# One fold for two units of attention in a graph-transformer kernel, and half of a weight matrix loaded behind the first input

## The chip, the cores and the metric

The kernel runs on one core of a Trainium2 chip. The metric is device time in microseconds of one launch; lower is better. The core's engines work side by side, each through its own instructions in order: TensorE (PE in the profile, its weight loads PEld) multiplies matrices into PSUM, VectorE (DVE) and ScalarE (ACT) work on elements and can read PSUM, [...], and SyncE (SP) issues nearly all DMA transfers. They wait for each other through semaphores.

## The reference, cut to what matters

For each of 16 samples, x has 1024 nodes of 256 channels; adj is a 1024 x 1024 matrix that all samples share. All is fp32.

```python
# layer 0: x = layernorm(x + attention)
c = mean(x, channels); A = 2 * abs(abs(sigmoid(c_j - c_i) - .5) - .5)
g = relu((x.T @ (adj * A)) * para)      # 256 x 1024: the queries, 4 heads of 64
k, v = split(x @ kv_w)
out = softmax(q @ k.T * scale) @ v
# layer 1: x = layernorm(x + (x + h) / 2)
h = relu(x @ w1_loop + adj @ (x @ w1_neigh) + b1)      # 128 wide
h = relu(h @ w2_loop + adj @ (h @ w2_neigh) + b2)      # 256 wide
```

The change touches the softmax's denominator: out is a sum over nodes of exp(score) * v, divided by the sum of the exponentials.

## The kernel before, in words

The loop over samples b (L1021) is a pipeline written out by hand: while sample b is in attention, the queries, keys and values of b+1 are made, the first graph convolution of b-1 and the second of b-2 run joined in one product, and the result of b-3 is normalized and stored. The order of the program text is the order of each engine's instructions (`tc.manual_schedule()`). Graph products, keys and values use a seven-product scheme in place of eight (a Strassen form), whose operands are sums and differences made by VectorE and GpSimd.

Attention (class at L602) of a sample is cut into four units: two pairs of heads by two halves of the nodes (512 queries). For a unit u:

- `scores(u)` (L616): eight tiles of keys, for each two matmuls (one for each head of the pair, L624) and one exp on ScalarE (L627, tile pr, 128 x 1024). VectorE adds the eight pr into acc (L631, L633), transposes it in blocks of 32 (L635, accB) and reduces it to den_part, 128 x 32 (L637). What is left is a sum over groups of partitions.
- `outputs(u)` (L639): sixteen matmuls of v with pr into one PSUM bank (av, L644), and a transpose into the tile o (L648).
- `add(u)` (L650): one matmul of the constant matrix `fold` with den_part (L656) finishes the sum for all partitions; two reciprocals, one for each head (L660); o times them (L662); o added to the residual stream xB (L664); sums of xB for the coming layer norm (L665). The last unit also joins these sums (L255) and takes the extremes of the reciprocals (L668, L669).

Where `add` stands differs by sample. With `both`, that is for samples 2 to 14, add(0) comes between scores(1) and outputs(1), ahead of the sums for the keys (L1081); add(1) after the second of seven graph products of the joined convolution (L1057, `between[2]`); add(2) after `c2.last()` and ahead of scores(3) (L1074); add(3) in the middle of step 1 of the query graph (L1147). Samples 0, 1 and 15 take them one unit later each, in the loop at L1091 or at set places.

After add(3) the same sample goes on with `norm.mean` in the middle of step 2 (fold of the sums on TensorE, L251; mean and subtraction on VectorE, L307 and L310), `norm.squares` (ScalarE, L315), and behind these `q.end` (L578): ScalarE copies the first of seven query products out of PSUM (L585), VectorE adds them up (L586 and on). Pair 3 of the query graph's right sides is made by VectorE (L495, L548 to L551) between add(3) and `norm.mean`. Then `kv.run` (L408) makes the keys and values of b+1; its first product on TensorE (L401) writes the PSUM buffer that L586 reads.

SBUF tiles of 128 x 1024 share a pool of 25 slots (`row_tile`, L99); a tile that finds no free slot waits for the last reader of another. The tile o has one slot of its own, so outputs(u+1) cannot write it before add(u) has read it. den_part has two slots. PSUM has three big buffers of two banks and two single banks (L85 to L92).

At the start (L115 to L120) x of sample 0 is loaded in four pieces by SP's queue, and kv_w as a whole, 512 KB, by ScalarE's queue at the same time. GpSimd makes sums of its blocks (L131), which SP stores; the keys of sample 0 (L343) need the left half of kv_w's columns, the values (L356) the right half.

Of the kernel before, what the change touches and what calls it, by code (L numbers as in the profile page):

```python
# [10 lines left out]
F32 = mybir.dt.float32  # L11
I32 = mybir.dt.int32
AF = mybir.ActivationFunctionType
ALU = mybir.AluOpType
# [4 lines left out]
def kernel(  # L19
# [31 lines left out]
    nc = tc.nc  # L51
# [39 lines left out]
    def bank_psum(name):  # L91
        return psum.tile([P, FB], F32, tag="bank", name=name, bufs=2)  # L92
# [20 lines left out]


    x_first = xpool.tile([P, NT, C], F32, tag="x", name="x_0")  # L115
    for t0 in range(0, NT, 2):
        nc.sync.dma_start(out=x_first[:, t0:t0 + 2, :],
                          in_=x[0, t0 * P:(t0 + 2) * P, :].rearrange("(t p) c -> p t c", p=P))
    kvw_sb = const.tile([P, NC, 2 * C], F32, name="kvw_sb")
    nc.scalar.dma_start(out=kvw_sb, in_=kv_w.rearrange("(cc p) f -> p cc f", p=P))  # L120
    w1l_sb = const.tile([P, NC, HID], F32, name="w1l_sb")
    w1n_sb = const.tile([P, NC, HID], F32, name="w1n_sb")
    w2l_sb = const.tile([HID, C], F32, name="w2l_sb")
# [172 lines left out]
    def by_node(t):  # L296
        return t.rearrange("p (bn r) -> p bn r", r=S)
# [304 lines left out]
    class Attention:  # L602
# [5 lines left out]

        def __init__(self, b, xB, qT, kT, v):
            self.b, self.xB, self.qT, self.kT, self.v = b, xB, qT, kT, v  # L610
            self.part, self.o = {}, {}

            self.rden = small.tile([P, len(UNITS) * FB // S], F32, tag="rden", name=f"rden_{b}", bufs=2)
            self.sums = small.tile([P, NC, NB], F32, tag="sums", name=f"sums_{b}", bufs=2)

        def scores(self, u):  # L616

            b, (pair, j) = self.b, UNITS[u]
            self.pr = []
            for mt in range(NT):  # L620
                ps = big_psum(f"s_{b}_{u}_{mt}")
                for s in range(2):
                    rows = slice(s * HD, (s + 1) * HD)
                    nc.tensor.matmul(ps[:, ts(s, FB)], self.kT[rows, pair, ts(mt, P)], self.qT[rows, pair, ts(j, FB)],  # L624
                                     start=True, stop=True)
                pr = row_tile(f"pr_{b}_{u}_{mt}")
                nc.scalar.activation(pr, ps, AF.Exp)  # L627
                self.pr.append(pr)
                if mt == 1:
                    acc = row_tile(f"acc_{b}_{u}")  # L630
                    nc.vector.tensor_add(acc, self.pr[0], pr)  # L631
                elif mt > 1:
                    nc.vector.tensor_add(acc, acc, pr)  # L633
            accB = row_tile(f"accB_{b}_{u}")
            nc.vector.transpose(accB, acc)  # L635
            self.part[u] = small.tile([P, N // S], F32, tag="den_part", name=f"den_part_{b}_{u}", bufs=2)
            nc.vector.tensor_reduce(self.part[u], by_node(accB), AX.X, ALU.add)  # L637

        def outputs(self, u):  # L639
            b, (pair, j) = self.b, UNITS[u]  # L640
            pav = bank_psum(f"av_{b}_{u}")
            for mt in range(NT):
                for s in range(2):
                    nc.tensor.matmul(pav[s * HD:(s + 1) * HD, :],  # L644
                                     self.v[:, mt, pair * P + s * HD:pair * P + (s + 1) * HD],
                                     self.pr[mt][:, ts(s, FB)], start=(mt == 0), stop=(mt == NT - 1))
            self.o[u] = work.tile([P, FB], F32, tag="o", name=f"o_{b}_{u}")
            nc.vector.transpose(self.o[u], pav)  # L648

        def add(self, u):  # L650

            b, (pair, j) = self.b, UNITS[u]
            half = FB // S
            pd = bank_psum(f"den_ps_{b}_{u}")
            den = pd[:, 0:2 * half]
            nc.tensor.matmul(den, fold.rearrange("p a k -> p (a k)"), self.part.pop(u), start=True, stop=True)  # L656
            rden = self.rden[:, ts(u, half)]
            for s in range(2):
                rows = slice(s * HD, (s + 1) * HD)
                nc.vector.reciprocal(rden[rows, :], den[rows, ts(s, half)])  # L660
            o = by_node(self.o.pop(u))
            nc.vector.tensor_mul(o, o, rden.unsqueeze(2).to_broadcast([P, half, S]))  # L662
            dst = by_node(self.xB[pair][:, ts(j, FB)])
            nc.vector.tensor_add(dst, dst, o)  # L664
            nc.vector.tensor_reduce(self.sums[:, pair, ts(j, half)], dst, AX.X, ALU.add)  # L665
            if u == len(UNITS) - 1:
                join(self.sums)
                nc.vector.tensor_reduce(rden_min[:, b:b + 1], self.rden, AX.X, ALU.min)  # L668
                nc.vector.tensor_reduce(rden_max[:, b:b + 1], self.rden, AX.X, ALU.max)  # L669
# [293 lines left out]
    def run():  # L963
# [57 lines left out]
        for b in range(B):  # L1021
# [29 lines left out]
            def gap1():  # L1051
                for t in (0, TJ):
                    q.load(t)
                if both:
                    both.fetch(1, 4)
                    both.run({1: (lambda: q.left(nc.gpsimd),),
                              2: (lambda: att.add(1),),  # L1057
                              6: (lambda: q.likeness(0), lambda: c3 and c3.moments()),
                              7: (lambda: q.likeness(TJ),),
                              5: (weigh_first,),  # L1060
                              4: (lambda: c3 and c3.finish(out[b - 3]),),
                              3: (c1.turn_blocks,)})
                else:
                    q.left(nc.gpsimd)
                    for t in (0, TJ):
                        q.likeness(t)
                    store("01", rows01)
                    c1.first(rows01, lambda: (att.add(1), adj_sums(rows01, 1), adj_sums(rows01, 2), weigh_first()))
                    c1.turn_blocks()

            def gap2():
                if both:
                    c2.last()
                    att.add(2)  # L1074

            between = [gap0, gap1, gap2] if c1 and more else []
            if more:
# [1 line left out]
            for u in range(len(UNITS)):  # L1079
                att.scores(u)  # L1080
                if u == 1 and between:  # L1081
                    att.add(0)
                    kv = KeysValues(b + 1, ready["xT"])
                    kv.sums()
                if u == 3 and between:
                    for t in (2, TJ + 2, 3, TJ + 3):
                        q.load(t)
                    for t in (2, TJ + 2, 3, TJ + 3):
                        q.likeness(t)
                    q.right(1)  # L1090
                if u and (not between or u == 3 and not both):  # L1091
                    att.add(u - 1)
                att.outputs(u)
                if u == 2 and more:
                    if c1:
                        for t in (1, TJ + 1):
                            q.load(t)
                            q.likeness(t)
                            q.times_adj(t)
                    else:  # L1100
                        for t in range(3):
                            q.load(t)
                            q.weigh(t)
                if u < 3 and between:
                    between[u]()
                if u == 0 and more and not between:
                    means(q, xb, str(b + 1))()
# [36 lines left out]
            elif more:  # L1144
                q.pair(2)
                q.step(0)
                q.step(1, lambda: att.add(3))  # L1147
                q.pair(3)
                q.step(2, lambda: (norm.mean(), norm.squares()))
                q.load_para()  # L1150
                kv.load()
                q.step(3)
                qT = q.end(norm.sum_squares)
                xB = load_blocked(b + 1, f"a{b + 1}")
                load_next()
                kT, v = kv.run(norm.variance, q.scale)
                if not c2:
                    adj_sums(rows01, 3)
                norm.scale()
                norm.spread()  # L1160
            else:
                c2.load_h1()
                c2.load_x()
                both.fetch(2, 3)
                c1.inner()
                both.left(nc.gpsimd)
                both.fetch(1, 4)
                both.run({1: (lambda: att.add(3),), 2: (norm.mean, norm.squares, norm.sum_squares), 7: (norm.variance,),
                          5: (norm.scale, norm.spread)})
                c1.turn(0)  # L1170
                c2.last()
                c1.turn(1)
# [86 lines left out]
```

## Time and profile before

| what | value |
|---|---|
| median of 3 runs | 2161.2 us (2160.72 to 2161.49) |
| the profiled execution's own time | 2160.7 us |
| span of the profiled execution | 2158.9 us, TensorE clock 0.998 |
| TensorE busy | 2145.5 us, 8412 records (two passes for each fp32 matmul) |
| VectorE busy | 1906.0 us, 2402 instructions |
| ScalarE busy | 1040.9 us |
| GpSimd busy | 361.7 us |
| fold of the denominators, L656 | 128 records for 64 matmuls, median 276 ns |
| one sample, first key product to the next one | 132.8 us (384.86 to 517.68 us) |

A profile line gives an engine, the line of the kernel, the operation, the tiles written and read, and times. The timeline gives start and duration in us, and in brackets the idle time of that engine ahead of the instruction with what ended it. A matmul's end is modelled and lies past the start of the next one, so distances between starts are the better measure of what TensorE spends.

### The profile page before, as it was taken

The numbers are of one execution on the slowest core, as the hardware profiler recorded it, in microseconds if no ns is written. First come the engines' busy times: TensorE is split into PE (matmuls) and PEld (weight loads), VectorE is DVE, ScalarE is ACT, GpSimd is POOL, SyncE is SP. The second block draws the span as 40 slices with busy tenths as digits, with TensorE's granted clock in tenths as the row PEclk, the third lists the DMA queues.
The fourth block names the chain that finished last, engine by engine and source line by source line (L and its number), as shares of the span: only waits on it lengthen the run. The fifth ranks groups of instructions, "written<-read, shape, count | busy, mean of one in ns | idle before, by whom it ended". The sixth has DMA issues, their size and how long they took to land.

```text
span 2158.9 us, 23875 instructions
## 1 busy us (share of the span) xinstructions
PE 2145.5 (99%) x8412; PEld 1030.9 (48%) x8412; DVE 1906.0 (88%) x2402; ACT 1040.9 (48%) x1374; POOL 361.7 (17%) x201
## 2 busy tenths in 40 slices
PE   9999999999999999999999999999999999999997
PEld 5344444544445444454545445454454544544354
DVE  5999998889998899998999989999889898889964
ACT  4745545545345554445544555445553445535412
POOL 1010130311303013030120302203021130211021
PEclk9999999999999999999999999999999999999999
DMA  9493653736548364563755636555374553733443
GB/s 236 120 145 117 147 156 108 160 113 123 160 118 181 93 126 151 138 170 88 121 172 124 159 88 121 172 127 156 98 130 153 127 156 118 140 133 83 122 136 99
DMA packets 611918, 290.72 MB, mean 135 GB/s; under 512 B 504784, under 2 KB 569168, under 8 KB 611792
## 3 DMA queue, kind: packets, MB, share of 16 engines
q1 hardware_dynamic: 611520, 288.61, 54.5%
q8 instruction: 68, 1.11, 0.2%
q14 instruction: 58, 0.48, 0.1%
q10 hardware_dynamic: 272, 0.52, 0.1%
HBM read 242.35 MB, written 46.72 MB: 134 GB/s over the span
## 4 chain that ended last, share of the span: by engine, by line


## 5 line engine op out<-in xcount | busy, mean ns | idle before, releaser
L627 ACT ACTIVATE pr<-s 128x1024 f32<-128x1024 f32 x512 | 476.1, 1054 | 183.8 <-PE s L624 183.0
L633 DVE TENSOR_TENSOR acc<-acc,pr 128x1024 f32<-128x1024 f32 x384 | 498.9, 1299 | 41.1 <-DVE acc L633 1.0
L624 PE MATMUL s<-qT,kT 64*128 64x512 f32 x2048 | 456.8, 596 | 0.0
L644 PE MATMUL av<-pr,v 128*64 128x512 f32 x2048 | 453.6, 595 | 0.0
L624 PEld LDWEIGHTS s<-qT,kT 64*128 64x128 f32 x2048 | 191.5, 186 | 232.9 <-ACT pr L627 112.8
L327 POOL TENSOR_TENSOR rstd<-rstd,neg_half 128x32 f32<-128x32 f32 x16 | 99.8, 6238 | 1129.8 <-DVE rstd L325 615.6
L644 PEld LDWEIGHTS av<-pr,v 128*64 128x64 f32 x2048 | 141.3, 137 | 289.3 <-issue 274.3
L489 ACT ACTIVATE wg<-c_row,c_col 128x1024 f32<-128x1024 f32 x128 | 147.0, 1148 | 69.1 <-DVE accB L635 50.5
L495 DVE SCALAR_TENSOR_TENSOR wg<-wg,adj 128x1024 f32<-128x1024 f32 x128 | 150.0, 1210 | 12.0 <-ACT wg L490 12.0
L922 PE MATMUL hu_ps<-adj,R 128*128 128x512 f32 x360 | 158.3, 596 | 0.0
L490 ACT ACTIVATE wg<-wg 128x1024 f32<-128x1024 f32 x128 | 135.4, 1058 | 4.1
L315 ACT ACTIVATE sq<-xB_a 128x1024 f32<-128x1024 f32 x32 | 33.8, 1057 | 197.0 <-DVE xB_a L310 195.7
L576 PE MATMUL g_ps<-wg,S 128*128 128x512 f32 x224 | 116.7, 603 | 0.0
L576 PE MATMUL g_ps<-T,S 128*128 128x512 f32 x224 | 114.4, 592 | 0.0
L576 PE MATMUL g_ps<-wg,x 128*128 128x512 f32 x224 | 109.0, 599 | 0.0
L922 PE MATMUL hu_ps<-adjT,t 128*128 128x512 f32 x240 | 105.7, 592 | 0.0
L922 PEld LDWEIGHTS hu_ps<-adj,R 128*128 128x128 f32 x360 | 67.3, 190 | 78.9 <-issue 78.7
L631 DVE TENSOR_TENSOR acc<-pr,pr 128x1024 f32<-128x1024 f32 x64 | 83.2, 1300 | 23.8 <-ACT pr L627 23.8
L938 ACT COPY snap<-hu_ps 128x512 f32<-128x512 f32 x15 | 8.8, 585 | 154.6 <-PE hu_ps L922 150.5
L635 DVE STREAM_TRANSPOSE accB<-acc 128x1024 f32<-128x1024 f32 x64 | 79.7, 1245 | 3.5 <-DVE acc L633 0.5
L637 DVE TENSOR_REDUCE den_part<-accB 128x32 f32<-128x1024 f32 x64 | 78.1, 1220 | 2.2
L810 PE MATMUL h_ps<-w2n_sb,uT 128*128 128x256 f32 x240 | 72.7, 385 | 0.0
(204 smaller groups left out, 3001.8 us busy)
## 6 DMA issues: line engine op xcount, KB each, us to landing
adj<-in_adj_dram SPq DMA_DIRECT2D x128, 512.0 KB, 4.6
adj<-adjT SPq DMA_DIRECT2D x120, 512.0 KB, 10.2
para<-in_L_gnn_para_dram SPq DMA_DIRECT2D x32, 512.0 KB, 3.5
xB_a<-in_x_dram SPq DMA_DIRECT2D x128, 128.0 KB, 4.3
x1d<-xB_a SPq DMA_DIRECT2D x128, 128.0 KB, 3.4
x<-x1d SPq DMA_DIRECT2D x16, 1024.0 KB, 15.0
xB<-in_x_dram SPq DMA_DIRECT2D x120, 128.0 KB, 4.7
x<-in_x_dram SPq DMA_DIRECT2D x15, 1024.0 KB, 6.4
```

Source lines behind the costliest of these rows:

```text
L327: nc.gpsimd.tensor_tensor(self.rstd, self.rstd, neg_half, ALU.pow)
L489: nc.scalar.activation(wg, self.c_row, AF.Abs, bias=self.c_col[:, t:t + 1], scale=-1.0)
L490: nc.scalar.activation(wg, wg, AF.Tanh, scale=-0.5)
L495: nc.vector.scalar_tensor_tensor(wg, wg, 1.0, self.adj.pop(t), op0=ALU.add, op1=ALU.mult)
L576: nc.tensor.matmul(self.p[n], x_n[:, k, :], w_n, start=(k == 0), stop=(k == TJ - 1))
L624: nc.tensor.matmul(ps[:, ts(s, FB)], self.kT[rows, pair, ts(mt, P)], self.qT[rows, pair, ts(j, FB)], start=True, stop=True)
L627: nc.scalar.activation(pr, ps, AF.Exp)
L631: nc.vector.tensor_add(acc, self.pr[0], pr)
L633: nc.vector.tensor_add(acc, acc, pr)
L635: nc.vector.transpose(accB, acc)
L644: nc.tensor.matmul(pav[s * HD:(s + 1) * HD, :], self.v[:, mt, pair * P + s * HD:pair * P + (s + 1) * HD], self.pr[mt][:, ts(s, FB)], start ...
L922: nc.tensor.matmul(dst, self.x[n][:, k, :], half_adj[w][:, k, :] if w else of_rows(rows, k), start=(start and k == 0), stop=(k == TJ - 1), ...
```

## The change

The fold takes two units at once, where a sample runs with the joined product (2 to 14). den_part becomes one tile for two units; add takes one or two units, with one matmul of 64 columns, two reciprocals over both units, and then per unit the product, the addition and the sums as before. add(0) and add(1) both stand where add(1) stood, add(2) and add(3) both where add(3) stood. As o of an even unit has to last longer, it moves to half of a row tile. In sample 1, add(0) now stands behind the sums for the keys. At the start kv_w is loaded in two halves: the keys' columns by ScalarE's queue as before, the values' columns by SP's queue, behind the four pieces of x.

```diff
+    kvw_sb = const.tile([P, NC, 2 * C], F32, name="kvw_sb")
     for t0 in range(0, NT, 2):
         nc.sync.dma_start(out=x_first[:, t0:t0 + 2, :],
                           in_=x[0, t0 * P:(t0 + 2) * P, :].rearrange("(t p) c -> p t c", p=P))
-    kvw_sb = const.tile([P, NC, 2 * C], F32, name="kvw_sb")
-    nc.scalar.dma_start(out=kvw_sb, in_=kv_w.rearrange("(cc p) f -> p cc f", p=P))
+    for eng, cols in (nc.scalar, slice(0, C)), (nc.sync, slice(C, 2 * C)):
+        eng.dma_start(out=kvw_sb[:, :, cols], in_=kv_w[:, cols].rearrange("(cc p) f -> p cc f", p=P))
...
-            self.part[u] = small.tile([P, N // S], F32, tag="den_part", name=f"den_part_{b}_{u}", bufs=2)
-            nc.vector.tensor_reduce(self.part[u], by_node(accB), AX.X, ALU.add)
+            if u % 2 == 0:
+                self.part = small.tile([P, 2, N // S], F32, tag="den_part", name=f"den_part_{b}_{u}", bufs=2)
+            nc.vector.tensor_reduce(self.part[:, u % 2, :], by_node(accB), AX.X, ALU.add)
+            self.parts[u] = self.part
...
-            self.o[u] = work.tile([P, FB], F32, tag="o", name=f"o_{b}_{u}")
+            name = f"o_{b}_{u}"
+            self.o[u] = work.tile([P, FB], F32, tag="o", name=name) if u % 2 else row_tile(name)[:, 0:FB]
             nc.vector.transpose(self.o[u], pav)
 
-        def add(self, u):
-
-            b, (pair, j) = self.b, UNITS[u]
-            half = FB // S
-            pd = bank_psum(f"den_ps_{b}_{u}")
-            den = pd[:, 0:2 * half]
-            nc.tensor.matmul(den, fold.rearrange("p a k -> p (a k)"), self.part.pop(u), start=True, stop=True)
-            rden = self.rden[:, ts(u, half)]
+        def add(self, *units):
+
+            b, half = self.b, FB // S
+            u0, n = units[0], len(units)
+            pd = bank_psum(f"den_ps_{b}_{u0}")
+            den = pd[:, 0:2 * half * n]
+            part = [self.parts.pop(u) for u in units][0]
+            nc.tensor.matmul(den, fold.rearrange("p a k -> p (a k)"),
+                             part[:, u0 % 2:u0 % 2 + n, :].rearrange("p u k -> p (u k)"), start=True, stop=True)
+            den = den.rearrange("p (u s h) -> p u s h", u=n, s=2)
+            rden = self.rden[:, u0 * half:(u0 + n) * half].rearrange("p (u h) -> p u h", u=n)
             for s in range(2):
                 rows = slice(s * HD, (s + 1) * HD)
-                nc.vector.reciprocal(rden[rows, :], den[rows, ts(s, half)])
-            o = by_node(self.o.pop(u))
-            nc.vector.tensor_mul(o, o, rden.unsqueeze(2).to_broadcast([P, half, S]))
-            dst = by_node(self.xB[pair][:, ts(j, FB)])
-            nc.vector.tensor_add(dst, dst, o)
-            nc.vector.tensor_reduce(self.sums[:, pair, ts(j, half)], dst, AX.X, ALU.add)
+                nc.vector.reciprocal(rden[rows], den[rows, :, s, :])
+            for k, u in enumerate(units):
+                pair, j = UNITS[u]
+                o = by_node(self.o.pop(u))
+                nc.vector.tensor_mul(o, o, rden[:, k, :].unsqueeze(2).to_broadcast([P, half, S]))
+                dst = by_node(self.xB[pair][:, ts(j, FB)])
+                nc.vector.tensor_add(dst, dst, o)
+                nc.vector.tensor_reduce(self.sums[:, pair, ts(j, half)], dst, AX.X, ALU.add)
...
-                              2: (lambda: att.add(1),),
+                              2: (lambda: att.add(0, 1),),
...
                 if both:
                     c2.last()
-                    att.add(2)
...
                 if u == 1 and between:
-                    att.add(0)
                     kv = KeysValues(b + 1, ready["xT"])
                     kv.sums()
...
-                if u and (not between or u == 3 and not both):
+                if u and (not between or u != 2 and not both):
                     att.add(u - 1)
...
-                q.step(1, lambda: att.add(3))
+                q.step(1, lambda: att.add(*((2, 3) if both else (3,))))
```

More of the change, by code (lines that the diff above doesn't have):

```diff
@@ L610, in __init__ @@
             self.b, self.xB, self.qT, self.kT, self.v = b, xB, qT, kT, v
-            self.part, self.o = {}, {}
+            self.parts, self.o = {}, {}
             self.rden = small.tile([P, len(UNITS) * FB // S], F32, tag="rden", name=f"rden_{b}", bufs=2)
```

## The prediction

> **What bounds the kernel now.** I read the page's busy times first, then the waits by engine, then the order of time around the four folds of one batch.
>
> ```profile
> PE 2145.5 (99%) x8412; PEld 1030.9 (48%) x8412; DVE 1906.0 (88%) x2402; ACT 1040.9 (48%) x1374; POOL 361.7 (17%) x201
> ...
> PE xT_ps L231 <- DMA x<-in_x_dram: 0.7, 1, 0.7
> PE k_ps L401 <- DVE U L586: 0.2, 1, 0.2
> ```
>
> TensorE is never idle but for the first microseconds and one wait of 0.2 us. So a matmul that goes is worth its place in TensorE's row, if nobody else is late by then. The second wait names the place where somebody nearly is: key product 1 (L401) writes a PSUM buffer that VectorE frees with L586. Next the timelines of batch 2 (a batch takes 132.8 us, and all thirteen of batches 2 to 14 look alike); columns are start, duration, engine, line, operation, tiles. TensorE first:
>
> ```profile
> 345.53 0.59 PE L812 MATMUL h_ps<-w2l_sb,h1T 128*128 128x256 f32 x2
> 345.96 0.30 PE L656 MATMUL den_ps<-den_part,fold 128*128 128x32 f32 x2
> 346.19 1.56 PE L624 MATMUL s<-qT,kT 64*128 64x512 f32 x6
> ...
> 369.82 0.30 PE L656 MATMUL den_ps<-den_part,fold 128*128 128x32 f32 x2
> ...
> 384.86 1.02 PE L401 MATMUL k_ps<-xT,kvw_sb 128*128 128x512 f32 x2
> ...
> 422.44 0.41 PE L656 MATMUL den_ps<-den_part,fold 128*128 128x32 f32 x2
> 422.78 1.94 PE L644 MATMUL av<-pr,v 128*64 128x512 f32 x8
> ```
>
> Starts tell the cost, since the modelled ends overlap: the fold of unit 0 (422.44) holds TensorE for 0.34 us, that of unit 2 (345.96) for 0.23. Each fold is one fp32 matmul in two passes, hence two records. Now VectorE and ScalarE, between the fold of unit 3 and that key product:
>
> ```profile
> 371.30 0.52 DVE L660 RECIPROCAL rden<-den_ps 64x16 f32<-64x16 f32 x2
> 371.85 0.69 DVE L662 TENSOR_TENSOR o<-o,rden 128x512 f32<-128x512 f32 x1
> 372.58 0.69 DVE L664 TENSOR_TENSOR xB_a<-xB_a,o 128x512 f32<-128x512 f32 x1
> 373.31 0.69 DVE L665 TENSOR_REDUCE sums<-xB_a 128x16 f32<-128x512 f32 x1
> 374.02 0.19 DVE L255 TENSOR_TENSOR sums<-sums 128x32 f32<-128x32 f32 x1
> ...
> 383.67 0.69 DVE L586 TENSOR_TENSOR U<-P,g_ps 128x512 f32<-128x512 f32 x1 [1.66 <-ACT P L585]
> ```
>
> ```profile
> 380.97 2.19 ACT L315 ACTIVATE sq<-xB_a 128x1024 f32<-128x1024 f32 x2 [12.74 <-DVE xB_a L310]
> 383.07 0.57 ACT L585 COPY P<-g_ps 128x512 f32<-128x512 f32 x1
> ```
>
> This is one chain without slack inside: reciprocals, the add of unit 3, join, pair 3 of the query graph (374.39 to 379.39), mean (L307, L310 to 382.01), the squares, the copy P behind them, L586, which ends at 384.36. The 1.66 us of idle time before L586 is no slack: the copy stands behind the squares, which stand behind VectorE's own L310. TensorE's key product comes at 384.86. Two more places calibrate the waits:
>
> ```profile
> 251.20 0.69 DVE L586 TENSOR_TENSOR U<-P,g_ps 128x512 f32<-128x512 f32 x1 [1.66 <-ACT P L585]
> ...
> 2057.90 0.52 DVE L660 RECIPROCAL rden<-den_ps 64x16 f32<-64x16 f32 x2 [2.10 <-PE den_ps L656]
> ```
>
> ```profile
> 251.94 1.13 PE L401 MATMUL k_ps<-xT,kvw_sb 128*128 128x512 f32 x2 [0.18 <-DVE U L586]
> ...
> 2057.55 0.30 PE L656 MATMUL den_ps<-den_part,fold 128*128 128x32 f32 x2
> ```
>
> In batch 1 TensorE did wait: L586 ended at 251.88, the product is shown at 251.94, and the values after it come 0.96 us later where 0.86 is usual, so 0.10 of weight load was exposed: a late key product really starts 0.16 us after L586's end. In batch 15 VectorE waited for a fold: reciprocals start 0.35 us after the fold's start.
>
> [...] passes of 128 columns follow each other by 112 ns (L405), and a fold between two full-array products costs 223 ns[...] (28 + 112 to the next product, and that one 512 to its successor in place of 429). [...] L633 takes 1.23 us alone and 2.1 beside GpSimd's additions. [...]
>
> **The change part by part.**
> TensorE, batches 2 to 14. The fold of unit 0 goes from between scores and outputs: the record before it has its 519 ns and the one after it its change of tile shape with or without it (331.93 has none), so the whole 0.338 us goes. The fold of unit 2 goes from between L812 and the scores: 28 + 206 ns; but a full-array pass just before scores costs 94 ns extra (523 in place of 429 at 324.3), which stays, so 0.140 goes. The folds of units 1 and 3 stay where they are with 64 columns, at the same 0.223. Sum 0.478 us a batch, 6.2 us in thirteen. Bounds: 0.45 to 0.48, if wider passes cost 27 ns each.
> VectorE, same batches. Unit 0's add moves behind the key sums (L385 to L388), o of unit 1 and L941. The work is the same less two reciprocals; VectorE's next idle time in that stage is 3.5 us at 325 in batch 2 and 0.68 us at 859.3 in later ones, which covers it. GpSimd's left side S now starts behind den_part of unit 1 (its row slot comes free there), so it slows the key sums and adds in place of the acc chain; S is wanted only at 360. With that cover gone it would be the 1 to 2 us of slower additions a batch.
> Unit 2's add moves from 348.56 to the add of unit 3. That frees acc of unit 3: its first addition needs the second pr, 349.31 less 0.48 = 348.83, so it starts at 348.88 in place of 351.17, and VectorE is done with pair 2 (L551 end 371.38) by about 369.1. But the fold stands at 369.82 - 0.478 = 369.34, so reciprocals start at 369.34 + 0.35 + 0.03 (64 columns) = 369.72, and VectorE idles 0.6 us. From there the chain is longer by one unit: 374.02 - 371.85 = 2.17, and 0.03 for wider reciprocals. L586 ends at 369.72 + (384.36 - 371.30) + 2.20 = 384.98. The key product can start at 385.14; TensorE would have been there at 384.86 - 0.478 = 384.38. It waits 0.76 us, and the batch is 0.28 us longer than before. Bounds: 0.15 to 0.45, from 0.1 either way on the waits' latency and the 64-column fold.
> Other takers of the late chain: T of pair 3 (L550, 378.67 + 0.62) is wanted by TensorE at 379.23, a wait of 0.2 us that is inside the 0.76 and not beside it; the fold of the sums at 375.58 finds join done at about 374.8; after the key product VectorE stands 0.35 us later against TensorE than before, and the nearest taker (key product 7, L433 done 391.34, wanted at 391.9) has 0.6.
> Slots and queues: an even unit's o now holds one of 25 row slots. The changed program's waits show what moves: ScalarE's likeness of tile 2 waits for accB of unit 3 (359.4, was 356.1), tile 6 follows and is done at 363.9, wanted at 365.2; the adjacency load of tile 6 goes out at 353.8, was 348.7, lands in 4.6 (page), wanted at 365.2. The load of far block 4 on the queue now waits for accB of unit 1, some 5 us later, wanted 15 us later. All cost nothing while these margins hold.
> Start. Half of kv_w (262 KB) goes from ahead of x to behind it:
>
> ```profile
> 6.10 2.13 PE L231 MATMUL xT_ps<-ident,x 128*128 128x128 f32 x12 [0.72 <-DMA x<-in_x_dram]
> 8.07 1.45 PE L351 MATMUL k_ps<-xT,kvw_sb 128*128 128x512 f32 x3
> ```
>
> x comes in four pieces of 256 KB; the later ones were ready at 6.09, 6.84 and 7.57, 0.74 us a piece, so x is about 0.7 us earlier (0 to 1.0), and TensorE is busy from there to 48.8. The values' half is wanted only at 15.4. The sync queue gets one issue more (0.5 us) ahead of eight adjacency loads, GpSimd's second half of sums and the store of them up to 1 us later; its late blocks are what L1005 waits for at 40.9, and VectorE has from 45.5 to about 47.4 before TensorE lets it go on. Cover gone: up to 1 us.
> Sum: 13 x 0.28 = +3.65, less 0.7: +2.95 us on a span of 2158.9. The profiled execution took 2160.7, the median of three is 2161.2, and I add the 2.95 to that: 2164.1 us, +0.14%. About 0.2% (4.3 us) is what a measurement of this kernel can tell from no change.
>
> **Rivals.** *The gain stands*: the chain has slack that I don't see, TensorE never waits, 13 x 0.478 + 0.7 = 6.9 us less, 2154.3. For it: TensorE's clean rows, VectorE's 12% idle. Against: batch 1, where the wait showed as soon as L586 was 0.4 us later. It decides if L586 ends before 384.2. *VectorE reaches the fold late*: the adjacency tile 6, sent 5 us later, or the likeness behind accB comes after 365.2, and the head start is lost. Beyond 0.6 us every bit is paid in full, thirteen times; with no head start (371.30) it is 1.58 us a batch, 20 us more, 2185. It is slower by the bound from 0.7 us of lateness. Against: 1.3 us margin for ScalarE, some 7 for the load. *Only the fold's saving and the chain, no start gain*: 2164.8.
>
> **How the numbers follow.** Forecast 0.76, own range 2161.8 to 2167 (0.15 to 0.45 a batch and the start's bounds), a quarter of it over 2165.5; gain stands 0.12; late VectorE 0.12, all slower. So faster 0.12, same 0.57, slower 0.31. The range 2159 to 2170 leaves out the first rival and most of the second.
>
> **What would show it.** 76 records of the fold in place of 128 (26 matmuls in two passes less); a wait of k_ps for U of 0.7 us thirteen times in TensorE's waits; idle time of VectorE for den_ps thirteen times; batches of 133.1 us; the first keys at 7.4. It is wrong if TensorE shows no such wait, if VectorE's reciprocals start more than 0.5 us after the fold, or if a new wait shows in the joined product.

## The result, and the profile after

The changed kernel takes 2163.77 us, the median of 22 runs (2162.86 to 2164.86); the kernel before took 2160.78 beside it (22 runs, 2160.16 to 2161.49). The ratio is 1.0014, 95% interval 1.0007 to 1.0020: 3.0 us slower, inside the 0.2% that the prediction called no change, though the interval leaves out 1. The profiled spans are 2161.6 and 2158.9 us. (What the prediction calls a batch is a sample here.)

The busy time of TensorE is the first line to look at, from the page of the changed kernel (time, share of the span, instructions; POOL is GpSimd):

```profile
PE 2146.5 (99%) x8360; PEld 1021.1 (47%) x8360; DVE 1904.5 (88%) x2350; ACT 1041.0 (48%) x1374; POOL 362.7 (17%) x201
```

TensorE has 52 records less and is still shown busy for 1.0 us more. Its busy time can't tell work from lateness here: a matmul whose weights come late is drawn longer (1.12 us in place of 1.02, below). The waits tell more. In this view of the changed kernel each line is engine, tile and line, then what it waited for; the numbers are us in total, times, and the longest. (Lines of the changed kernel stand 1 to 9 further down: L401 is L402, L550 is L551, L586 is L587, L656 is L661, L660 is L667, L662 is L671. U is the sum of query products that L586 makes, T a right side of the query graph.)

```profile
PEld k_ps L402 <- DVE U L587: 15.4, 14, 1.2
DVE rden L667 <- PE den_ps L661: 14.2, 14, 2.5
PEld g_ps L577 <- DVE T L551: 13.9, 25, 0.9
...
PE k_ps L402 <- DVE U L587: 3.8, 14, 0.4
```

Before the change the same waits were these (the prediction shows that of PE for U, 0.2 us):

```profile
PEld k_ps L401 <- DVE U L586: 4.8, 14, 1.0
...
PEld g_ps L576 <- DVE T L550: 3.6, 14, 0.5
...
DVE rden L660 <- PE den_ps L656: 2.1, 1, 2.1
```

Before, the matmul's wait for U was there once, 0.2 us; now it is there fourteen times, in sample 1 and in each of samples 2 to 14. VectorE's wait for the fold was there once, in sample 15, and is now there in samples 2 to 14 as well. The wait of the weight loads for T has grown from 3.6 us to 13.9. The sums of PEld are not losses: a weight load can run ahead under the matmul before it (before the change, that of key product 1 of sample 2 starts 0.43 us ahead of its own matmul), and its idle time counts from its own predecessor. What it costs is read from the distances between matmuls, in the timeline of TensorE, changed kernel, with sample 0's start and sample 2 (start, duration, engine, line, operation, tiles, idle time before):

```profile
4.88 2.77 PE L232 MATMUL xT_ps<-ident,x 128*128 128x128 f32 x16
7.49 2.74 PE L352 MATMUL k_ps<-xT,kvw_sb 128*128 128x512 f32 x6
...
344.63 0.59 PE L821 MATMUL h_ps<-w2l_sb,h1T 128*128 128x256 f32 x2
345.16 2.85 PE L625 MATMUL s<-qT,kT 64*128 64x512 f32 x12
...
368.79 0.33 PE L661 MATMUL den_ps<-den_part,fold 128*128 128x64 f32 x2
...
378.83 1.12 PE L577 MATMUL g_ps<-T,S 128*128 128x512 f32 x2
...
384.52 1.12 PE L402 MATMUL k_ps<-xT,kvw_sb 128*128 128x512 f32 x2 [0.27 <-DVE U L587]
```

The first keys come at 7.49 instead of 8.07. The fold between the product L821 and the scores is gone. From the fold of the denominators to key product 1 it is now 15.73 us, where it was 384.86 - 369.82 = 15.04. Two products in that stretch are drawn 1.12 us in place of 1.02, and these are the late ones: between the starts of the matmuls, 0.26 us is lost at 378.83 (586 and 533 ns where 429 are usual) and 0.54 us at 384.52 (863 and 533). The records show only 0.27 us of idle time for the second, since the matmul before it is drawn 0.16 us past its 429 ns.

VectorE over the same stretch, changed kernel:

```profile
369.16 0.72 DVE L667 RECIPROCAL rden<-den_ps 64x32 f32<-64x32 f32 x2 [0.87 <-PE den_ps L661]
369.92 0.69 DVE L671 TENSOR_TENSOR o<-o,rden 128x512 f32<-128x512 f32 x1
...
371.97 0.68 DVE L671 TENSOR_TENSOR o<-o,rden 128x512 f32<-128x512 f32 x1
...
374.14 0.19 DVE L256 TENSOR_TENSOR sums<-sums 128x32 f32<-128x32 f32 x1
...
378.10 0.68 DVE L551 TENSOR_TENSOR T<-wg,T 128x512 f32<-128x512 f32 x1
...
383.78 0.69 DVE L587 TENSOR_TENSOR U<-P,g_ps 128x512 f32<-128x512 f32 x1 [1.66 <-ACT P L586]
```

The two adds now stand one behind the other, and both behind a fold for which VectorE waits 0.87 us. L587 ends at 384.47, and TensorE goes on 0.05 us later. Measured from one key product to the next, a sample takes 133.14 us (133.2 in two of the thirteen), before 132.82. The first key product of sample 1 stands at 251.38, before at 251.94; that of sample 14 at 1982.36, before at 1978.71. So the start gives 0.56 us, thirteen samples take 4.2, and 3.65 is left, of which the profiled span shows 2.7: the stretch from the last matmul's start to the end of the program is 10.0 us here and 11.0 before. Among the twelve profiled kernels of this study it lies between 9.4 and 11.4, though no edit touches the program there, so it is left out of the readings below. It seems to go with the kernel and not with the single execution: the median less the last matmul's start in the trace is 11.2 us where the stretch is 9.4, 11.9 to 12.4 where it is 9.9 to 10.5, and 12.7 to 12.9 where it is 11.0 or more. So differences of about 1 us between medians come from there, at least in part; what makes them is not known.

### The profile page after: what moved, and what is told of

The parts are those of the page before. It is cut to its first block, busy times and chain, and to the rows that moved or that the text cites. A ratio compares the mean times of both kernels' runs of the same rounds, so it can differ in the third digit from the quotient of the medians.

```text
span 2161.6 us, 23756 instructions
## 1 busy us (share of the span) xinstructions
PE 2146.5 (99%) x8360; PEld 1021.1 (47%) x8360; DVE 1904.5 (88%) x2350; ACT 1041.0 (48%) x1374; POOL 362.7 (17%) x201
## 4 chain that ended last, share of the span: by engine, by line
## 5 line engine op out<-in xcount | busy, mean ns | idle before, releaser
L634 DVE TENSOR_TENSOR acc<-acc,pr 128x1024 f32<-128x1024 f32 x384 | 487.2, 1269 | 40.8 <-DVE acc L634 0.5
```

## The experiments

The theory: TensorE saves 0.478 us a sample, and the joined fold of units 2 and 3 makes the chain from reciprocals to U 2.2 us longer, so TensorE waits for T and U. Rivals: the loss lies in the wide folds themselves; in the first pair, or in the row slot that o takes; in the start. The table has all runs; "a sample" is the usual distance between key products, which shows less scatter than the medians. "Before" is the kernel before on the same chip.

| kernel | median, us | before, us | ratio (95% interval) | a sample, us |
|---|---|---|---|---|
| before | | | | 132.82 |
| the change | 2163.77 | 2160.78 | 1.0014 (1.0007 to 1.0020) | 133.14 |
| start alone | 2159.91 | 2160.61 | 0.9997 (0.9988 to 1.0005) | 132.82 |
| folds alone | 2164.22 | 2160.27 | 1.0018 (1.0011 to 1.0026) | 133.14 |
| units 0 and 1 alone | 2154.22 | 2160.61 | 0.9972 (0.9961 to 0.9982) | 132.48 |
| units 2 and 3 alone | 2168.08 | 2160.27 | 1.0036 (1.0022 to 1.0049) | 133.48 |
| o in a row tile, on before | 2160.13 | 2160.76 | 0.9997 (0.9989 to 1.0005) | 132.82 |
| one sum twice, on before | 2165.85 | 2160.61 | 1.0024 (1.0015 to 1.0034) | 133.19 |
| squares later | 2157.35 | 2160.27 | 0.9985 (0.9979 to 0.9992) | 132.60 |
| squares later, on before | 2159.47 | 2160.76 | 0.9993 (0.9985 to 1.0002) | 132.82 |
| fold early | 2153.39 | 2160.61 | 0.9967 (0.9955 to 0.9979) | 132.34 |
| fold early, squares later | 2153.80 | 2160.27 | 0.9970 (0.9957 to 0.9982) | 132.34 |

**The start and the folds apart.** The kernel before with kv_w in two halves:

```diff
-    nc.scalar.dma_start(out=kvw_sb, in_=kv_w.rearrange("(cc p) f -> p cc f", p=P))
+    for eng, cols in (nc.scalar, slice(0, C)), (nc.sync, slice(C, 2 * C)):
+        eng.dma_start(out=kvw_sb[:, :, cols], in_=kv_w[:, cols].rearrange("(cc p) f -> p cc f", p=P))
```

> The kernel before with nothing but kv_w in two halves, the values' half behind x. The theory (x comes earlier by the half that no longer runs beside it, and TensorE is busy from there on): first keys and all later work about 0.6 us earlier (the changed kernel's key product of sample 1 stood at 251.38 us, before at 251.94), so about 2160.2 us. The rival (the later loads on the sync queue give it back): 2160.8 us or more.

And the changed kernel with kv_w as one load, the same diff read backwards:

> The changed kernel with kv_w loaded as a whole again, so only the folds change. The chain theory: the start's half alone was worth 0.7 us and does not meet the folds, so 2164.4 us, 3.6 over before. A rival in which the start's half is paid back later, by the late load of the values' columns: 2163.0 or less.

The first takes 0.7 us off the median, which its interval can't tell from nothing; its key product of sample 1 stands at 251.54, 0.40 us earlier than before. In all five kernels that have the two halves and leave the order of ScalarE alone, that product stands at 251.38 to 251.57; in the four with one load, at 251.94 to 252.06. The second is 4.0 us over before, where 3.6 was expected, with samples of 133.14 us as in the changed kernel and that product at 252.06. The start's part is a gain of about half a microsecond, seen in the traces and too small for the medians, and it doesn't meet the folds.

**The two pairs apart.** First the changed kernel with units 2 and 3 as before:

```diff
                     c2.last()
+                    att.add(2)
...
-                q.step(1, lambda: att.add(*((2, 3) if both else (3,))))
+                q.step(1, lambda: att.add(3))
```

> The changed kernel with units 0 and 1 folded together, units 2 and 3 apart as before. The theory (the loss is made by the chain that starts at the fold of units 2 and 3): 0.338 us a sample off TensorE, thirteen times, 4.4 us, and 0.6 us from the start, no wait of the key product for U beyond the one of sample 1: about 2155.8 us. The rival (the even units' o in row tiles, and with it later loads, make the loss): the wait or others stay, about 2160 us or more.

Then the changed kernel with only units 2 and 3 joined:

```diff
-                              2: (lambda: att.add(0, 1),),
+                              2: (lambda: att.add(1),),
...
                 if u == 1 and between:
+                    if both:
+                        att.add(0)
```

> The changed kernel, but units 0 and 1 have folds and adds of their own at their old places; only units 2 and 3 are joined. The chain theory: each sample loses the 0.34 us that unit 0's fold gave back and keeps the longer chain, 13 x 0.66 = 8.6 us over before, less 0.6 at the start: 2168.7 us. If part of the loss came from units 0 and 1 (their adds moved, the row slot of o), it would be 2167 or less.

A sample takes 132.48 us in the first, 0.34 less than before, which is the 0.338 worked out for unit 0's fold from the starts around it. In the second it takes 133.48, 0.66 more than before, the 0.32 of the changed kernel and the 0.34 that it gives up. So the first pair earns its full saving, and all of the loss sits in the second, whose median is 7.8 us over before where 8.0 was expected. The first median lies 1.6 us under its expectation; up to the key product of sample 14 the trace shows 4.9 us of the 6.4, and the rest of its shorter span lies behind the last matmul (9.4 us there), in the stretch left out above.

**The row slot.** The kernel before, with o as in the change:

```diff
-            self.o[u] = work.tile([P, FB], F32, tag="o", name=f"o_{b}_{u}")
+            name = f"o_{b}_{u}"
+            self.o[u] = work.tile([P, FB], F32, tag="o", name=name) if u % 2 else row_tile(name)[:, 0:FB]
```

> The kernel before, with o of even units in half of a row tile, as in the changed kernel; four folds a sample as before. The chain theory: the slot moves transfers and ScalarE's likeness by some us inside their margins, TensorE waits for none of it, 2160.8 us within 0.5. A rival in which the slots carry a part of the loss: 3 us or more over before.

A sample takes 132.82 us, as before. With four folds the row slot costs nothing, and the early fold below, which keeps the slot, gets the whole saving.

**The chain made longer by itself.** If a longer chain is the loss, any work put into it must cost what goes beyond the time to spare. The kernel before, with the sums of unit 3 made twice (the second writes over the first):

```diff
-            nc.vector.tensor_reduce(self.sums[:, pair, ts(j, half)], dst, AX.X, ALU.add)
+            for _ in range(2 if u == 3 and 2 <= b < B - 1 else 1):
+                nc.vector.tensor_reduce(self.sums[:, pair, ts(j, half)], dst, AX.X, ALU.add)
```

> The kernel before with the sums of unit 3 reduced twice in samples 2 to 14: one more VectorE instruction of 0.72 us between the fold and the key product, none for TensorE. The theory (before, the key product had 0.34 us to spare, 0.0 in two samples): 11 x 0.38 + 2 x 0.72 = 5.6 us more, about 2166.4 us, and a wait of the key product for U. The rival (VectorE, busy 88%, hides 0.72 us there): 2160.8 us.

The timeline of this kernel in sample 2, VectorE and then TensorE (its lines behind L665 stand one further down than before):

```profile
373.33 1.41 DVE L666 TENSOR_REDUCE sums<-xB_a 128x16 f32<-128x512 f32 x2
...
384.41 0.69 DVE L586 TENSOR_TENSOR U<-P,g_ps 128x512 f32<-128x512 f32 x1 [1.66 <-ACT P L585]
...
385.15 1.13 PE L401 MATMUL k_ps<-xT,kvw_sb 128*128 128x512 f32 x2
```

The sums take 1.41 us in place of 0.69, U is later by the same 0.7, and the key product shows the longer form of a late one. A sample takes 133.19 us, 0.37 more than before. The expectation's 5.6 us, 0.43 a sample, was a little large: 5.2 by the medians, 5.1 up to the key product of sample 14. It counted samples 3 and 12 as having nothing to spare, since U ended only 0.16 us ahead in them before; here they are like the others, and sample 10 alone takes longer, 133.55 us. For the usual sample the prediction's own figures give the measured one: L586 ended 0.50 us ahead of the product and may end 0.16 ahead, so 0.34 of the 0.71 is free. One more instruction of VectorE a sample, which gives TensorE no work, costs 5 us on the kernel.

**The end of the chain taken off.** In the changed kernel ScalarE's copy P stands behind the squares, and these behind VectorE's L311, though P itself needs neither. Here the squares go behind the copy:

```diff
-                q.step(2, lambda: (norm.mean(), norm.squares()))
+                q.step(2, norm.mean)
...
-                qT = q.end(norm.sum_squares)
+                qT = q.end(lambda: (norm.squares(), norm.sum_squares()))
```

> The changed kernel with ScalarE's squares behind the copy P, so the copy no longer stands in the chain behind the mean. The chain theory: key product 1 no longer waits for U (0.43 us idle and 0.10 of weight load gone), but the wait for T of pair 3 stays (0.16 and 0.10 us a sample), so a sample takes 0.22 us less than before: 2160.8 - 2.8 - 0.6 = 2157.4 us. A rival in which the loss is in the wide folds themselves: 2163.8, as the changed kernel. A rival in which removing the last wait frees everything: 2154.

And the same edit on the kernel before, to see what it is worth alone:

> The kernel before, with the squares behind the copy P. The chain theory: before, U ended ahead of the key product's turn in samples 2 to 14, so the move takes away only sample 1's wait (0.2 us and 0.1 of weight load): 2160.5 us. If the move were a gain of its own, which would spoil the reading of it on the changed kernel (6.4 us there), it would be 2155 to 2159 here.

The timeline of the first, sample 2, ScalarE, VectorE and TensorE, and then its one line of waits for T:

```profile
379.94 0.59 ACT L586 COPY P<-g_ps 128x512 f32<-128x512 f32 x1 [12.49 <-PE g_ps L577]
...
381.99 0.68 DVE L587 TENSOR_TENSOR U<-P,g_ps 128x512 f32<-128x512 f32 x1
...
378.78 1.12 PE L577 MATMUL g_ps<-T,S 128*128 128x512 f32 x2
...
384.04 1.02 PE L402 MATMUL k_ps<-xT,kvw_sb 128*128 128x512 f32 x2
```

```profile
PEld g_ps L577 <- DVE T L551: 14.1, 26, 0.8
```

P is copied ahead of the squares, and U follows the mean at once, with no idle time: it ends 1.4 us before its taker. The key product is back to its usual form. The product from T at 378.78 is still late, and a sample takes 132.60 us: of the 0.80 us that TensorE lost, the 0.54 in front of the key product are gone and the 0.26 in front of T have stayed, as expected. So there were two waits on one chain. On the kernel before, the move leaves the sample at 132.82 and takes only 0.35 us from sample 1 and 0.11 from sample 2; it is no gain of its own there. (Its median lies 1.3 us under before, where 0.3 was expected, and its interval can't tell that from nothing.)

**The start of the chain moved ahead.** Last, the whole joined add goes ahead of step 1 of the query graph, so that VectorE finds the fold done:

```diff
-                q.step(1, lambda: att.add(*((2, 3) if both else (3,))))
+                if both:
+                    att.add(2, 3)
+                q.step(1, None if both else lambda: att.add(3))
```

> The changed kernel with the fold of units 2 and 3 ahead of step 1 of the query graph in place of its middle: VectorE's order is the same. The theory (VectorE idled 0.9 us for the fold, and the chain behind it ends 0.79 us late): VectorE starts the reciprocals as soon as it is done with pair 2, the key product waits no more, thirteen times 0.478 us and 0.6 us are gained: about 2154.0 us. The rival (the wait has another cause, a load or a slot): VectorE ends no earlier, about 2163.8 us.

And the same with the squares later as well:

> The changed kernel with the fold of units 2 and 3 ahead of step 1 and the squares behind the copy P. The chain theory: with the early fold alone U already ended 0.4 us ahead of its need, so more slack buys nothing but sample 1's 0.1 us: 2153.3 us, within 0.3 of the early fold alone (2153.4). If the early fold still left hidden waits, 2152.5 or less.

The timeline of the first, sample 2, TensorE and VectorE:

```profile
365.54 0.33 PE L661 MATMUL den_ps<-den_part,fold 128*128 128x64 f32 x2
...
384.01 1.02 PE L402 MATMUL k_ps<-xT,kvw_sb 128*128 128x512 f32 x2
...
368.39 0.72 DVE L667 RECIPROCAL rden<-den_ps 64x32 f32<-64x32 f32 x2
...
383.00 0.69 DVE L587 TENSOR_TENSOR U<-P,g_ps 128x512 f32<-128x512 f32 x1 [1.66 <-ACT P L586]
```

The fold stands 2.85 us ahead of the reciprocals, which start behind pair 2 without idle time; U ends at 383.69, 0.32 us ahead of its taker. In samples 2 to 14 the lateness at T and U is gone, but for 0.1 us in sample 5, and the usual sample takes 132.34 us: 0.48 less than before, the whole of the two folds. At 2153.39 us this kernel takes 7.2 us less than the one before on the same chip, and so less than the change. With the squares later too, every sample takes 132.34: TensorE has no more lateness here to give back. The median of that kernel is not lower but 0.4 us higher, on another chip; up to the key product of sample 14 its trace is 0.5 us shorter, and the stretch behind the last matmul is 0.9 us longer.

## Why the prediction was right

The forecast was 2164.1 us, and 2163.8 was measured. Its mechanism is the one that the runs show; going through its steps:

- **The saving on TensorE**, 0.338 and 0.140 us a sample. Right: 0.34 with the first pair alone, 0.48 with both where nothing is late. That a fold of 64 columns costs no more than one of 32 was an estimate, as the kernel before has none of 64. It was right too, or the 0.48 could not be whole: in sample 2, from the start of the fold in step 1 of the query graph to that of the second product behind it, it is 1.08 us with either (369.82 to 370.90 before, 368.79 to 369.87 after).
- **VectorE waits for the fold.** Right in kind: reciprocals start 0.37 us after the fold's start, where 0.38 was worked out. It waits 0.87 us in sample 2 (0.58 to 0.94 in the others) and not 0.6: pair 2 was done 0.25 us earlier than reckoned. This costs nothing, as the fold is the later of the two.
- **The chain grows by 2.20 us.** Measured 2.26 from the start of the reciprocals to the end of U (15.31 against 13.05), but its two terms were both off. The reciprocals were given 0.03 us more, an estimate, and take 0.21 more from start to the product behind them (0.76 against 0.55). The second unit was given 2.17 and takes 2.05 (369.92 to 371.97): its product, which reads nothing that the instruction before it wrote, starts 0.60 us after it, where 0.72 is the distance inside a unit. They nearly cancel; the 0.06 left over is part of why a sample costs 0.32 and not 0.28.
- **The wait of 0.76 us**, measured 0.80, with 0.26 of it at T, inside the sum and not beside it, as the prediction had it. The sign named for it, a wait of 0.7 us of k_ps for U, shows as 0.27 us only; the rest is in matmuls drawn longer. That the T wait is a taker of its own shows only when the later one is removed: the squares' move got back 0.54 and not 0.80.
- **The start, 0.7 us**: 0.56 by the key product of sample 1. The load ran as predicted, the first keys at 7.49 with 7.4 forecast, and the wait for x is gone from TensorE; the four pieces of x land in 4.0 us, the median, where it was 4.9.
- **Slots, queues, GpSimd's sums** at no cost: no wait of TensorE for them appears, and the row slot alone left the sample at 132.82.
- **All thirteen samples alike.** Not quite: before, U ended 0.50 us ahead of the key product in most, but 0.43 in sample 8 and 0.16 in samples 3 and 12, which had nothing to spare. This made no difference here, as in the changed kernel the chain starts at the fold, whenever VectorE is done with pair 2.
- **The sum**: 13 x 0.28 - 0.7 = +2.95. By the traces it is 4.2 - 0.56 = +3.65 at sample 14, by the medians +3.0. That the medians' 3.0 meets the forecast's 2.95 so closely is luck: the samples cost half a microsecond more than forecast, the start gave 0.14 less, and the stretch behind the last matmul, which the prediction doesn't reckon with, took about 0.7 of it back. (By its own bounds the prediction's range begins at 2162.2, not 2161.8: 2161.2 + 13 x 0.15 - 1.0.)

Of the rivals, the gain that stands (2154.3) fell by U, though it is nearly what the early fold reaches. VectorE late at the fold fell by the 0.87 us. The changed folds with no start gain (2164.8) lie too near the forecast for the medians to decide; the traces show the start's gain, and the folds alone, without it, took 2164.2.

## What to carry to other kernels

When work is taken off the busy engine, look for the chain on another engine that is nearly as late: joining two small operations also joins what stands behind them, and here 0.48 us saved on TensorE cost 0.80 in waits for VectorE. Before joining, write down for each taker how far ahead of need its input is done (here 0.5 us, 0.34 of it free), and compare that with what the joined part puts in front of it. If the join is worth having, issue it earlier, so that its result waits for the engine and not the engine for it.

## What had not been expected of the hardware

A reciprocal over 32 columns takes about 0.10 us more than one over 16. The operations on the tile den_ps (instructions, then ns min/median/max, and first and last start in us) show it, first before and then after:

```profile
L660 DVE RECIPROCAL rden<-den_ps x128: 211/254/263, 79.5 to 2058.2; 64x16 f32<-64x16 f32 x128
```

```profile
L667 DVE RECIPROCAL rden<-den_ps x76: 209/349/361, 78.9 to 2061.9; 64x32 f32<-64x32 f32 x52, 64x16 f32<-64x16 f32 x24
```

The medians mix the reciprocals of the two heads, and in the second also 24 narrow ones. Form by form the difference is a little larger: in sample 2 the two take 243 and 260 ns before and 350 and 360 after, so 100 to 107 ns for 16 columns, 6.3 to 6.7 ns a column. The prediction's estimate of 0.03 us for both is about 1 ns a column, the slope of VectorE's additions in these traces (0.19 us for 32 columns, 0.69 for 512, so 1.04 ns a column); that of the reciprocal is six times as steep. (The wide form reads two stretches of 16 columns, with a gap between them, and no run tells what that costs by itself.) Two reciprocals of 32 columns still cost less than four of 16 (0.72 us against 1.04), but on a chain that sets the end it is the 0.2 us that count.
